# A graph network's residual layer: one gather table first and the other behind it, rows turned early, and the last node batches rearranged

## The chip, the cores and the metric

The kernel runs on one core of a Trainium2 chip. The core has engines that run beside each other, each with its own queue of instructions: PE multiplies matrices (PEld is its loading of weights), DVE works on vectors, ACT evaluates functions and copies, POOL here issues gathers (indirect DMAs), SP issues the other DMAs. The metric is the device time of one execution in microseconds (us); lower is better.

## The reference, cut to what matters

There are 6250 nodes of 128 features and 100000 edges, sorted by destination.

```python
msg_in = jnp.concatenate([node_features[src], node_features[dst], edge_features], axis=1)
h = jax.nn.silu(msg_in @ mW1 + mb1)
messages = h @ mW2 + mb2
aggregated = jax.ops.segment_sum(messages, dst, num_segments=N)
upd_in = jnp.concatenate([node_features, aggregated], axis=1)
u = jax.nn.silu(upd_in @ uW1 + ub1)
updated = u @ uW2 + ub2
return layer_norm(node_features + updated, ln_g, ln_b)
```

The output is `layernorm(x + that)`.

## The kernel before

**Tables.** The first matrix of an edge's message acts on three pieces: the source's features, the destination's features and four edge attributes. So the kernel makes two tables over all nodes: A (`tab_a`), x times the first half of mW1, and B (`tab_b`), x times the second half plus the bias. The nodes are 49 tiles of 128; `parts` puts eight tiles in a part, six full parts and one of a single tile. For each part, `turn_x` transposes x on PE (line 321) and ACT copies the result to `xT` (line 322); then, for four tiles at a time, PE multiplies with both halves at once (line 336, 256 columns), ACT copies A's half to a buffer `t` of which there are two (line 338), DVE adds the bias to B's half and writes it over x (line 339), and SP writes both to memory (lines 342 and 343). The PSUM tiles of this stage come from a pool `wide` of three. After the loop come the destination lists (`destination_lists`, lines 211 to 251: transposes on PE, small DVE work, flags) and edge attributes.

**Edges.** Edges are worked on in 98 groups of 1024 (the last has 672), eight tiles of 128 each. `fetch` has POOL issue one gather for each tile of a group (line 268). The gathered rows lie in a ring `gath` of AHEAD + 2 = 6 buffers, and POOL takes them in order of the groups. The first RAW = 4 groups gather rows of x itself, since no table is there yet; from group 4 on rows of A are gathered, which must wait for all of A.

For a group g the edge loop does this:

- SP loads a window of 96 rows of B and the four attribute rows (`load`, lines 525 and 526): the matrix `mv` and the lower rows of `st`.
- DVE writes the upper rows of `st`, a one-hot of the destination (`node_matrix`, line 530), and `oh`, the same by edges (`edge_matrix`, line 543).
- PE multiplies `st` and `mv` (`products`, line 555), which gives B's and the attributes' share.
- From group 4 on, DVE adds the gathered A rows (`hidden`, line 575) and ACT applies silu (line 576). For the first four groups `hidden` transposes the raw rows on PE (line 568), DVE copies them out (line 570), and `products` multiplies them with the first half of mW1 beside line 555 (line 559); ACT applies silu straight from PSUM (line 571). A raw buffer of the ring is free as soon as line 568 has read it.
- PE sums h over the destinations with `oh` (`by_nodes`, lines 582 and 585), and DVE adds that to `acc` and to the counts `deg` (`add`, line 591).

PE, DVE, ACT and SP run their instructions in the order in which the program writes them (`manual_schedule`).

**Nodes.** `node_batch` is a generator that carries a batch of node tiles through the update and both norms in steps, one step per group; `advance` moves all running batches by one step. A batch starts once the sums of its nodes are complete. The tiles are cut from the front into eleven batches of four, one of three, and a last one of two, which alone waits for the final group:

```python
for i0, n in groups(NT - 2, BT):
    batches.append((i0, n, (i0 + n) * P * E // (N * GE) + 1))
batches.append((NT - 2, 2, NG))
```

In a batch ACT copies its part of `acc` and `deg` (lines 433 and 435), PE multiplies (438 to 440), ACT applies silu (443), PE multiplies again (445, 454), and DVE and ACT do the two norms (456 to 483; the square root is line 425). Silu and square root lie in different function tables of ACT, which have to be loaded at each switch. In the last iterations both running batches take their steps in turn, the older one first.

Of the kernel before, what the change touches and what calls it, by code (L numbers as in the profile page):

```python
# [18 lines left out]
P = 128  # L19
# [5 lines left out]
def kernel(  # L25
# [46 lines left out]
    G = 8  # L72
# [24 lines left out]
    def groups(n, g):  # L97
        return [(i, min(g, n - i)) for i in range(0, n, g)]


    batches = []
    for i0, n in groups(NT - 2, BT):
        batches.append((i0, n, (i0 + n) * P * E // (N * GE) + 1))
    batches.append((NT - 2, 2, NG))

    edges = ExitStack()
    edges.enter_context(tc.manual_schedule(engines={ENG.SP, ENG.PE, ENG.DVE, ENG.Activation}))
# [210 lines left out]
    def turn_x(i0, n):  # L318
        pt = wide()
        for i in range(n):  # L320
            nc.tensor.transpose(pt[:, i, :], x_sb[:, i0 + i, :], ident)
        nc.scalar.copy(xT[:, i0 * P : (i0 + n) * P], pt[:, :n, :].rearrange("p i f -> p (i f)"))

    parts = groups(NT, G)
    turn_x(*parts[0])
    for k, (i0, n) in enumerate(parts):
        if k + 1 < len(parts):
            turn_x(*parts[k + 1])

        tb = x_sb[:, i0 : i0 + n, :]  # L330
        ta = tpool.tile([P, G, H], F32, name="t", bufs=2)
        for j0, m in groups(n, G // 2):
            pm = wide().rearrange("p (i s) f -> p i s f", s=2)
            for j in range(m):
                cols = slice((i0 + j0 + j) * P, (i0 + j0 + j + 1) * P)
                nc.tensor.matmul(pm[:, j], xT[:, cols], w1, start=True, stop=True)  # L336
            own = slice(j0, j0 + m)
            nc.scalar.copy(ta[:, own], pm[:, :m, 0, :])
            nc.vector.tensor_add(
                tb[:, own], pm[:, :m, 1, :], b1[:, None, :].to_broadcast([P, m, H])  # L340
            )
        nc.sync.dma_start(by_node(tab_b)[:, i0 : i0 + n, :], tb)
        nc.sync.dma_start(by_node(tab_a)[:, i0 : i0 + n, :], ta[:, :n])
        cols = slice(i0 * P, NW if i0 + n == NT else (i0 + n) * P)
        nc.vector.memset(acc[:, cols], 0.0)
        nc.vector.memset(deg[:, cols], 0.0)
# [3 lines left out]
    destination_lists()  # L350
    attribute_rows(0)
    destinations(0)
    if E < NG * GE:
        pad = tpool.tile([ED, NG * GE - E], F32, name="pad")
        nc.vector.memset(pad, 0.0)
        nc.sync.dma_start(ea_d[:, E:], pad)
# [42 lines left out]
        nc.scalar.copy(mb2u, pm[0:1, 2, :])  # L399


    def node_batch(i0, n, work, new, y):

        cols = slice(i0 * P, (i0 + n) * P)
        m = (min((i0 + n) * P, N) - i0 * P) // n
        assert m * n == min((i0 + n) * P, N) - i0 * P

        def rows_of(t):

            return t[i0 * P : i0 * P + m * n].rearrange("(p j) f -> p j f", j=n)  # L410

        def flat(t):
            return t[:, :n].rearrange("p i f -> p (i f)")

        def moments(v):
            mv = work.tile([P, BT, 2], F32, name="mv", bufs=2)
            for i in range(n):
                st = work.tile([P, 6], F32, name="st", bufs=2)
                nc.vector.bn_stats(st, v[:, i, :])  # L419
                nc.vector.bn_aggr(mv[:, i, :], st)  # L420
            return mv

        def std(mv):
            r = work.tile([P, BT], F32, name="r", bufs=2)
            nc.scalar.activation(r[:, :n], mv[:, :n, 1], AF.Sqrt, bias=eps)  # L425
            return r

        xs = new("xs")
        if m < P:
            nc.vector.memset(xs[m // 32 * 32 :, :n], 0.0)  # L430
        nc.sync.dma_start(xs[:m, :n], rows_of(x))
        acc_b = new("acc_b")
        nc.scalar.copy(flat(acc_b), acc[:, cols])
        deg_b = new("deg_b", 1)
        nc.scalar.copy(flat(deg_b), deg[:, cols])
        yield
        y = y()
        nc.tensor.matmul(flat(y), u1x, xT[:, cols], start=True, stop=False)
        nc.tensor.matmul(flat(y), w2u, flat(acc_b), start=False, stop=False)
        nc.tensor.matmul(flat(y), mb2u, flat(deg_b), start=False, stop=True)  # L440
        yield
        uT = new("uT")
        nc.scalar.activation(flat(uT), flat(y), AF.Silu, bias=ub1_col)
        yield
        nc.tensor.matmul(
            y[:, :n],
            ones[0:1, :],
            ub2_row[:, None, :].to_broadcast([1, n, H]),
            start=True,
            stop=False,  # L450
        )
        by_p = flat(uT).rearrange("k (p j) -> k p j", j=n)
        for i in range(n):
            nc.tensor.matmul(y[:, i, :], by_p[:, :, i], u2, start=False, stop=i == n - 1)  # L454
        yield
        nc.vector.tensor_add(y[:, :n], y[:, :n], xs[:, :n])
        mv = moments(y)
        nc.vector.tensor_add(xs[:, :n], xs[:, :n], b_b[:, None, :].to_broadcast([P, n, H]))
        yield
        r = std(mv)  # L460
        yield
        nc.vector.reciprocal(r[:, :n], r[:, :n])
        z = new("z")
        for i in range(n):
            nc.vector.scalar_tensor_tensor(  # L465
                y[:, i, :], y[:, i, :], mv[:, i, 0:1], g_b, op0=OP.subtract, op1=OP.mult
            )
            nc.vector.scalar_tensor_tensor(  # L468
                z[:, i, :], y[:, i, :], r[:, i : i + 1], xs[:, i, :], op0=OP.mult, op1=OP.add
            )  # L470
        mz = moments(z)
        yield
        rz = std(mz)
        yield
        nc.vector.reciprocal(rz[:, :n], rz[:, :n])
        shift = work.tile([P, BT], F32, name="shift", bufs=2)
        nc.vector.scalar_tensor_tensor(  # L477
            shift[:, :n], mz[:, :n, 0], -1.0, rz[:, :n], op0=OP.mult, op1=OP.mult
        )
        yield  # L480
        o = z
        for i in range(n):
            nc.scalar.activation(  # L483
                o[:, i, :], z[:, i, :], AF.Identity, bias=shift[:, i : i + 1], scale=rz[:, i : i + 1]
            )
        yield
        nc.sync.dma_start(rows_of(out), o[:m, :n])
# [60 lines left out]
        )  # L548
        return oh

    def products(g, xg=None):
        pre = rows_ps()
        st = stbuf[g % NST].rearrange("k (i c) -> k i c", i=G)
        for i in range(tiles_of(g)):
            nc.tensor.matmul(  # L555
                pre[:, i, :], st[:, i, :], mv[g % NM], start=True, stop=xg is None
            )
            if xg is not None:
                nc.tensor.matmul(pre[:, i, :], xg[:, i, :], w1[:, 0, :], start=False, stop=True)  # L559
        return pre  # L560

    def hidden(g):
        h = hbuf[g % NH]
        ga = rows.pop(g)
        if g < RAW:
            px = rows_ps()
            for i in range(G):
                nc.tensor.transpose(px[:, i, :], ga[:, i, :], ident)  # L568
            xg = work.tile([P, G, P], F32, name="s")
            nc.vector.tensor_copy(xg, px)  # L570
            nc.scalar.activation(h, products(g, xg), AF.Silu)  # L571
        else:
            n = tiles_of(g)
            s = work.tile([P, G, H], F32, name="s")
            nc.vector.tensor_add(s[:, :n], ga[:, :n], pre.pop(g)[:, :n])  # L575
            nc.scalar.activation(h[:, :n], s[:, :n], AF.Silu)  # L576
        return h

    def by_nodes(g, h, oh):
# [14 lines left out]
        load(g)  # L594
    for g in range(MADE):
        node_matrix(g)
    pre, oh, h, pt, running = {}, {0: edge_matrix(0)}, {}, {}, []
    for g in range(NG + 1):
        if g == 3:
            load_weights()  # L600
        if g == 5:
# [7 lines left out]
            fetch(g + AHEAD)  # L609
        if g + LEAD < NG:  # L610
            load(g + LEAD)
        if g == RAW:
            for k in (g, g + 1):
                pre[k] = products(k)
        last = g >= NG - 1
        if not last:
            h[g] = hidden(g)
        if g >= RAW and g + 2 < NG:
            pre[g + 2] = products(g + 2)
        if g + MADE < NG:  # L620
            node_matrix(g + MADE)
# [4 lines left out]
                add(k, pt.pop(k))  # L626
        if not last:
            pt[g] = by_nodes(g, h.pop(g), oh.pop(g))
        for i0, n, first in batches:
            if g == min(first + 1, NG):  # L630
                tiles = node_tiles(nodes, node_y)
                if first == NG:

                    tiles = (
                        nodes,
                        lambda name, p=P: gath.tile([P, G, H], F32, name="ga")[:p, :BT],
                        lambda: rows_ps()[:, :BT],
                    )
                running.append(node_batch(i0, n, *tiles))
        advance(running)  # L640
        if g >= NG - 2:
            advance(running)
        if g == NG - 1:
            pt[g] = by_nodes(g, hidden(g), oh.pop(g))
    while running:
        advance(running)
    edges.close()
# [155 lines left out]
```

## Time and profile before

| what | us |
|---|---|
| median of three runs | 1023.12 (1022.43 to 1024.61) |
| the profiled execution's own time | 1023.03 |
| its span, first to last instruction | 1021.3 |
| POOL busy in it | 741.8 |
| PE busy | 685.0 |
| DVE busy | 477.2 |
| ACT busy | 238.2 |
| end of the raw gathers on POOL | 43.94 |
| first gather from A | 52.24 |
| last gather issued | 992.31 |
| last output issued | 1015.68 |

All times in the text are counted from the start of the span. The page's groups have one row for each line of the kernel, engine and operation, with busy time, mean duration and the idle time before it. A wait is named with the instruction that waited and the one that ended it.

### The profile page before, as it was taken

To read this page: it belongs to the slowest core of one execution; us is meant where nothing else is said; L and a number is where in the kernel's file an instruction comes from. 1 tells how busy PE (TensorE), PEld (TensorE's weight loads), DVE (VectorE), ACT (ScalarE), POOL (GpSimd) and SP (SyncE) were. 2 spreads that over 40 slices of the span, in tenths; PEclk is the share of its full clock that TensorE was granted. 3 is DMA by queue.
4 is the path that set the end of the run, shared out by engine and by line. 5 is a ranking of instruction groups with operands and counts; after the bars stand their busy time and mean duration, and the time that the engine had idled before them with its cause. 6 is when DMAs were issued, how large, how long until landed. Compare 5 with 4: busy or idle time off the path is not lost.

```text
span 1021.3 us, 11233 instructions
## 1 busy us (share of the span) xinstructions
PE 685.0 (67%) x3696; PEld 618.4 (61%) x3696; DVE 477.2 (47%) x1018; ACT 238.2 (23%) x294; POOL 741.8 (73%) x790
## 2 busy tenths in 40 slices
PE   5748896658667677657547765767667666647763
PEld 4637886547556676556546664666666565647652
DVE  3752765434534444542543453452544453453454
ACT  2311231221231131131222232122222132123134
POOL 6577777777777777777777777777777777777760
PEclk9957997686587657767787777767767767776665
DMA  8943342232323322323233224233232332222220
GB/s 214 288 118 93 90 116 58 77 92 75 86 74 84 83 78 55 93 77 94 60 90 87 65 66 110 62 90 83 68 86 73 85 84 71 75 78 68 53 57 31
DMA packets 69916, 88.95 MB, mean 87 GB/s; under 512 B 20671, under 2 KB 51534, under 8 KB 69850
## 3 DMA queue, kind: packets, MB, share of 16 engines
q0 software_dynamic: 25024, 51.30, 20.0%
q1 hardware_dynamic: 41290, 35.08, 11.9%
q10 hardware_dynamic: 3536, 1.77, 0.7%
q8 instruction: 31, 0.51, 0.2%
q14 instruction: 35, 0.29, 0.1%
HBM read 76.71 MB, written 11.38 MB: 86 GB/s over the span
## 4 chain that ended last, share of the span: by engine, by line
POOL 53%; issue 24%; DMA 7%; DVE 6%; PE 4%; ACT 1%; DVEq 0%; POOLq 0%; ACTq 0%
POOL ga L268 53%; DMA ga<-tab_a,src_i 7%; PE pt L585 1%; PE pre L555 1%; DVE st L530 1%; DVE z L468 1%; DVE oh L543 1%; DVE y L465 1%; PE pre L559 1%; DVE st L419 1%; DVE mv L420 1%; PE pre L568 0%; DVE s L570 0%; ACT h L571 0%; DVE s L575 0%
## 5 line engine op out<-in xcount | busy, mean ns | idle before, releaser
L268 POOL DMA_INDIRECT ga<-tab_a,src_i x750 | 710.5, 947 | 237.9 <-issue 216.7
L555 PE MATMUL pre<-mv,st 100*128 100x128 f32 x1564 | 319.0, 382 | 277.3 <-DVE s L575 223.9
L555 PEld LDWEIGHTS pre<-mv,st 100*128 100x128 f32 x1564 | 293.2, 286 | 299.0 <-DVE s L575 243.0
L575 DVE TENSOR_TENSOR s<-ga,pre 128x1024 f32<-128x1024 f32 x94 | 114.4, 1217 | 469.7 <-DMA ga<-tab_a,src_i 450.5
L576 ACT ACTIVATE h<-s 128x1024 f32<-128x1024 f32 x94 | 99.1, 1055 | 661.7 <-DVE s L575 661.6
L585 PE MATMUL pt<-oh,h 128*128 128x96 f32 x1564 | 247.9, 326 | 5.5 <-ACT h L571 5.5
L585 PEld LDWEIGHTS pt<-oh,h 128*128 128x128 f32 x1564 | 243.5, 245 | 12.4 <-ACT h L571 6.6
L530 DVE TENSOR_SCALAR_CACHE_REDUCE st<-near,p_next 96x1024 f32<-96x1024 uint8 x98 | 124.2, 1269 | 1.7 <-DMA ea_d<-pad 1.7
L543 DVE TENSOR_TENSOR oh<-w_row,rel 128x768 f32<-128x768 f32 x98 | 92.9, 948 | 0.0
L582 PE MATMUL pt<-ident,deg_g 96*1 96x96 f32 x98 | 32.0, 327 | 9.1 <-DVE deg L591 8.9
L425 ACT ACT_TABLE_LOAD x24 | 30.8, 1283 | 2.7 <-DVE mv L420 2.3
L454 PEld LDWEIGHTS y<-u,uT 128*128 128x128 f32 x94 | 22.7, 327 | 10.4 <-issue 10.4
L268 POOL DMA_INDIRECT ga<-in_x_dram,src_i x24 | 22.6, 944 | 7.3 <-issue 7.3
L576 ACT ACT_TABLE_LOAD x21 | 26.9, 1283 | 0.4
L591 DVE TENSOR_TENSOR acc<-acc,pt 128x96 f32 x98 | 23.6, 241 | 4.9 <-PE pt L585 4.9
L454 PE MATMUL y<-u,uT 128*128 128x128 f32 x94 | 25.8, 429 | 0.0
L336 PE MATMUL wide<-w,xT 128*128 128x256 f32 x98 | 24.1, 403 | 0.0
L591 DVE TENSOR_TENSOR deg<-deg,pt 1x96 f32 x98 | 23.1, 235 | 0.0
L336 PEld LDWEIGHTS wide<-w,xT 128*128 128x128 f32 x98 | 19.5, 205 | 2.9
L420 DVE BATCH_NORM_AGGREGATE mv<-st 128x2 f32<-128x6 f32 x98 | 17.8, 182 | 3.4
L483 ACT ACTIVATE z<-z,shift,r 128x128 f32<-128x128 f32 x47 | 19.2, 479 | 0.4 <-DVE shift L477 0.4
L559 PE MATMUL pre<-w,s 128*128 128x128 f32 x64 | 16.0, 341 | 4.8 <-DVE s L570 4.8
(117 smaller groups left out, 343.2 us busy)
## 6 DMA issues: line engine op xcount, KB each, us to landing
ga<-tab_a,src_i POOLq DMA_INDIRECT x750
near<-near_d SPq DMA_DIRECT2D x24, 384.0 KB
mv<-tab_b SPq DMA_DIRECT2D x98, 48.0 KB
tab_b<-x_sb SPq DMA_DIRECT2D x6, 512.0 KB
tab_a<-t SPq DMA_DIRECT2D x6, 512.0 KB
xs<-in_x_dram SPq DMA_DIRECT2D x11, 256.0 KB
out_dram<-z SPq DMA_DIRECT2D x11, 256.0 KB
st<-ea_d SPq DMA_DIRECT2D x98, 16.0 KB
```

Source lines behind the costliest of these rows:

```text
L268: nc.gpsimd.indirect_dma_start(out=rows[g][:, i, :], out_offset=None, in_=x if g < RAW else tab_a[:, :], in_offset=bass.IndirectOffsetOnAx ...
L336: nc.tensor.matmul(pm[:, j], xT[:, cols], w1, start=True, stop=True)
L425: nc.scalar.activation(r[:, :n], mv[:, :n, 1], AF.Sqrt, bias=eps)
L454: nc.tensor.matmul(y[:, i, :], by_p[:, :, i], u2, start=False, stop=i == n - 1)
L530: nc.vector.tensor_scalar(stbuf[g % NST][:W], near.pop(g), p_next, 0.0, op0=OP.is_equal, op1=OP.add, accum_out=deg_g[:, g : g + 1],)
L543: nc.vector.tensor_tensor(oh, w_row[:, None, :].to_broadcast([P, G, W]), rel[:, g, :, None].to_broadcast([P, G, W]), op=OP.is_equal,)
L555: nc.tensor.matmul(pre[:, i, :], st[:, i, :], mv[g % NM], start=True, stop=xg is None)
L575: nc.vector.tensor_add(s[:, :n], ga[:, :n], pre.pop(g)[:, :n])
L576: nc.scalar.activation(h[:, :n], s[:, :n], AF.Silu)
L582: nc.tensor.transpose(pt[0:1, W:], deg_g[:, g : g + 1], ident[:W, :W])
L585: nc.tensor.matmul(pt[:, :W], h[:, i, :], oh[:, i, :], start=i == 0, stop=i == n - 1)
L591: nc.vector.tensor_add(at, at, of)
```

## The change

It has four parts.

1. The loop over parts makes only A, 128 columns a tile. Destination lists and attributes follow, and then a second loop makes B for all parts.
2. In that second loop, `turn_rows` transposes the raw rows of groups 0 to 3 and writes them back over the gathered rows. `products` reads them from there, and the raw groups' products are made two groups ahead, like the others'.
3. The batches are cut so that the first has one tile, eleven have four, and the last two have two each. From NG - 6 on, all running batches take two steps in a group.
4. After the loop the last batch (`final`) reads `acc` and `deg` directly, and goes ahead of the batch before it in every round of steps.

```diff
+    LAST = 2
     batches = []
-    for i0, n in groups(NT - 2, BT):
+    first = (NT - 2 * LAST) % BT
+    for i0, n in [(0, first)] * (first > 0) + [
+        (first + i, n) for i, n in groups(NT - 2 * LAST - first, BT)
+    ] + [(NT - 2 * LAST, LAST)]:
         batches.append((i0, n, (i0 + n) * P * E // (N * GE) + 1))
-    batches.append((NT - 2, 2, NG))
+    batches.append((NT - LAST, LAST, NG))
...
+    def table(i0, n, half):
+        pm = wide()
+        for j in range(n):
+            cols = slice((i0 + j) * P, (i0 + j + 1) * P)
+            nc.tensor.matmul(pm[:, j, :], xT[:, cols], w1[:, half, :], start=True, stop=True)
+        return pm[:, :n, :]
+
+    def turn_rows(g):
+
+        px = wide()
+        for i in range(G):
+            nc.tensor.transpose(px[:, i, :], rows[g][:, i, :], ident)
+        nc.vector.tensor_copy(rows[g], px)
+
     turn_x(*parts[0])
     for k, (i0, n) in enumerate(parts):
         if k + 1 < len(parts):
             turn_x(*parts[k + 1])
-
-        tb = x_sb[:, i0 : i0 + n, :]
         ta = tpool.tile([P, G, H], F32, name="t", bufs=2)
-        for j0, m in groups(n, G // 2):
...
-        nc.sync.dma_start(by_node(tab_b)[:, i0 : i0 + n, :], tb)
+        nc.scalar.copy(ta[:, :n], table(i0, n, 0))
         nc.sync.dma_start(by_node(tab_a)[:, i0 : i0 + n, :], ta[:, :n])
...
     destinations(0)
+    for k, (i0, n) in enumerate(parts):
+        if k < RAW:
+            turn_rows(k)
+
+        tb = x_sb[:, i0 : i0 + n, :]
+        nc.vector.tensor_add(tb, table(i0, n, 1), b1[:, None, :].to_broadcast([P, n, H]))
+        nc.sync.dma_start(by_node(tab_b)[:, i0 : i0 + n, :], tb)
...
-        acc_b = new("acc_b")
-        nc.scalar.copy(flat(acc_b), acc[:, cols])
-        deg_b = new("deg_b", 1)
-        nc.scalar.copy(flat(deg_b), deg[:, cols])
+        sums, counts = acc[:, cols], deg[:, cols]
+        if not final:
+
+            acc_b, deg_b = new("acc_b"), new("deg_b", 1)
+            nc.scalar.copy(flat(acc_b), sums)
+            nc.scalar.copy(flat(deg_b), counts)
+            sums, counts = flat(acc_b), flat(deg_b)
...
-    def products(g, xg=None):
+    def products(g):
         pre = rows_ps()
         st = stbuf[g % NST].rearrange("k (i c) -> k i c", i=G)
         for i in range(tiles_of(g)):
...
+            nc.tensor.matmul(pre[:, i, :], st[:, i, :], mv[g % NM], start=True, stop=g >= RAW)
+            if g < RAW:
+                nc.tensor.matmul(
+                    pre[:, i, :], rows[g][:, i, :], w1[:, 0, :], start=False, stop=True
+                )
         return pre
...
-    pre, oh, h, pt, running = {}, {0: edge_matrix(0)}, {}, {}, []
-    for g in range(NG + 1):
+    oh, h, pt, running = {0: edge_matrix(0)}, {}, {}, []
+    pre = {g: products(g) for g in range(2)}
+    for g in range(NG):
...
-        if g >= RAW and g + 2 < NG:
+        if g + 2 < NG:
             pre[g + 2] = products(g + 2)
...
+        for _ in range(2 if g >= NG - 6 else 1):
+            if not last:
+                advance(running)
+
+    g = NG - 1
+    advance(running)
+    before = running[-1]
+    next(before)
+    pt[g] = by_nodes(g, hidden(g), oh.pop(g))
+    next(before)
+    add(g, pt.pop(g))
+    final = node_batch(
...
+        final=True,
+    )
+    for _ in range(2):
+        next(final)
+    running = [final, before] + running[:-1]
     while running:
         advance(running)
```

## The prediction

> **What bounds the kernel now.** I read the page's chain of waits first, then its groups, then the waits of POOL alone, then the timeline of the first 125 us and of the last 50.
>
> ```profile
> POOL 53%; issue 24%; DMA 7%; DVE 6%; PE 4%; ACT 1%; DVEq 0%; POOLq 0%; ACTq 0%
> L268 POOL DMA_INDIRECT ga<-tab_a,src_i x750 | 710.5, 947 | 237.9 <-issue 216.7
> ...
> POOL ga L268 <- DMA mv<-in_L_gnn_mW_dram: 8.3, 1, 8.3
> POOL ga L268 <- PE pre L568: 1.5, 1, 1.5
> ```
>
> POOL issues 782 gathers, 0.944 us each and 0.30 to the next: 1.25 us, 977 us in all, nearly the whole span. From 4 us on it stops only twice for more than 0.5 us: 8.29 us until table A has landed, and 1.46 us (1.16 more than the usual 0.30) until buffer 3 of its ring of six is free. So the time is: when POOL starts group 6 (the first group that reuses a buffer) + 92 groups + the tail after the last gather. I price the change in these terms.
>
> ```profile
> 43.00 0.94 POOL L268 DMA_INDIRECT ga<-in_x_dram,src_i  x1 [0.30 <-issue]
> 52.24 0.94 POOL L268 DMA_INDIRECT ga<-tab_a,src_i  x1 [8.29 <-DMA mv<-in_L_gnn_mW_dram]
> ...
> 72.21 0.94 POOL L268 DMA_INDIRECT ga<-tab_a,src_i  x1 [0.30 <-issue]
> ...
> 994.99 0.95 DVE L575 TENSOR_TENSOR s<-ga,pre 128x768 f32<-128x768 f32 x1 [0.18 <-DMA ga<-tab_a,src_i]
> ...
> 1000.84 0.26 DVE L591 TENSOR_TENSOR acc<-acc,pt 128x96 f32 x1 [4.90 <-PE pt L585]
> ...
> 1009.48 0.43 DVE L456 TENSOR_TENSOR pre<-pre,ga 128x256 f32<-128x256 f32 x1
> ...
> 1015.34 0.34 SPq L487 DMA_DIRECT2D out_dram<-ga  x1
> ```
>
> The reader sees the raw gathers end at 43.94, the tables' gap, group 6 at 72.21 with no wait (buffer 0 was freed by the transposes of line 568 at 56.87 to 58.84), and a tail of 20 us after the last data.
>
> **What the skill says.** "TensorE: Matmul & The Clock Gate", Part 1: the PE runs at half clock until a free-running window of 3413 ns has been busy. The trace agrees: the clock is 0.50 or 1.00, and in half-microsecond slices it switches near 47.87, 71.77, 75.18 and 88.84, whole multiples of 3.41 apart. Its Part 4 says of transposes that the full clock does not engage for them. The trace has one stretch that tests this, the first line here (columns: the stretch, its length, then PE, PEld, DVE, ACT and POOL busy, clock, DMA share, GB/s):
>
> ```profile
> 78.20:81.60 3.40, 3.26 (x16) 2.97 (x15) 0.53 (x1) 0.00 (x0) 2.54 (x3) 0.50 0.23 57
> 81.60:85.00 3.40, 2.65 (x12) 2.65 (x13) 2.76 (x4) 0.00 (x0) 2.49 (x4) 0.50 0.14 40
> 85.00:88.40 3.40, 3.40 (x18) 3.40 (x17) 0.00 (x0) 0.00 (x0) 2.51 (x3) 0.50 0.21 58
> 88.50:92.00 3.50, 2.47 (x20) 2.18 (x20) 0.00 (x0) 2.00 (x2) 2.76 (x3) 0.95 0.23 58
> ```
>
> 78.2 to 81.6 was 96% busy, over half of it transposes (79.1 to 81.0), and the clock stayed at half; 85.0 to 88.4, matmuls alone and busy throughout, raised it. That supports the page, with one sample. "DMA: Bandwidth & Descriptors", Anatomy of one DMA, gives about 2.0 us fixed for a transfer; here an st load issued until 63.07 lets PE go at 65.07. "ScalarE: Activation LUTs", What ACT_TABLE_LOAD costs, gives 1283 ns; the page's 24 loads have that mean.
>
> **Part 1: A alone in the first loop.** Before, a part of 8 tiles takes PE 1.04 (transposes) + 3.32 (256 columns) and the parts follow at 4.33 us. At 128 columns a tile takes 0.22 at full clock, 0.43 at half (the pairs of lines 555/559 at 72 and 68 us), so a part takes 1.04 + 1.75 = 2.8. The first A runs at half clock to 20.1 as now; five more periods end PE's share near 34 instead of 43.6. ACT has two copies of 1.01 a part and keeps up. An A tile's buffer waits for the write two parts back: 512 KB at some 235 GB/s (287 moved from 24 to 43.6 us, less 52 for gathers of 64 KB in 1.25 us) is 2.2 + 2.0 us, with the copy some 5.4 for two parts, no limit. The last A is then issued near 38 and lands near 40.5, before POOL comes at 44.25. **The 8.29 gap falls to 0.30: -8.0**, and groups 4 and 5 end at 64.2.
>
> **Part 2: what group 6 waits for now.** In the changed order of instructions POOL's first gather of group 6 waits for PE and DVE: raw rows are turned in place, so buffer 0 is read until the last matmul of products(0). That needs mv, which needs all of B. Before, it needed only line 568. The chain:
> - The destination lists come to PE at 34 instead of 48.65, with the same 8.2 us to the last small transpose (48.65 to 56.87): 42. DVE's memsets and subtracts are done by then; bad_i ends 3.3 us later, 45.7, batches one longer (0.15).
> - The B stretch is 4 x 8 transposes and 49 matmul tiles on PE: 4 x 1.04 + 49 x 0.22 = 14.9 at full clock, 4 x 1.91 + 49 x 0.43 = 28.7 at half. It starts cold (idle since 36). DVE has 4 copies and 7 adds of some 1.2 (line 570; two adds of 0.65 before) and is under PE.
> - Turns and tables alternate: 1.91 of transposes, 3.42 of matmuls. If transposes count as busy, PE is at full clock after at most two windows: end near 59. If they don't, a window needs 3.0 to 3.4 us of pure matmuls out of a period of 5.3, and gets it only by phase; surely only in parts 4 to 6, which have no turns: end near 69.
> - From there 1.3 to the last big add, then its 512 KB behind the write before: 4.5 to 5.5. SP's mv and st issue and land in 2.85 (62.27 to 65.07 and the wake). products(0) is 16 tiles, PE cold again: 6.0 (between 3.5 and 6.8).
> - Sum: 59 + 1.3 + 5 + 2.85 + 6 = 74 at best, 69 + 1.3 + 5 + 2.85 + 6 = 84. I take 80: the window may fit by phase in the middle of the stretch.
>
> Group 6 then starts at 80 instead of 72.21: **+7.8**, of which -1.3 comes back: the waits of 1.16 at 93.33 and 0.17 at 113.47 go, as products(1) to (3) follow within POOL's 10 us a group. **Net start +6.5**, range -1.5 (T = 72) to +13. Queued behind the waiting gather are only later gathers, and their data are not missed: PE, DVE and ACT still have groups 0 to 5 to work through. But POOL never catches up what it stood, since every group costs it 10 us to the end.
>
> SP is moved past nothing it waits long for: mv, ea, near_d stand between A and B, all issued by 46, the first B at 48. The middle of the loop costs nothing: POOL runs five buffers ahead there, some 40 us of cover.
>
> **Part 3: the tail.** Before: h of group 97 at 997.40 behind four z activations, pt until 1000.8, then two ACT copies of 0.41 and 0.40, silu behind two table loads (1004.77), matmuls to 1007.66, and DVE reaches the last batch only at 1009.48, held by the three-tile batch. After: acc and deg feed PE directly, two tiles instead of three, silu of the last batch ahead of the other's sqrt. From the waits of the order: h(96) pays one table load of 1.28 behind its s, since the load carries that wait; the middle batch's y ends near 995.8 (3 x 0.63), its second matmuls near 998.2, pt(97) at 1000.6, add 0.3, two matmuls 1.3, silu 1002.3, matmuls 1005.1. The middle batch's sqrt follows with a load, 1004.4, its normalisation 2.45: 1006.9. So DVE takes the last batch at 1007.0 (now 1009.48), 6.35 to the output instead of 5.86, for the shared engine: 1013.35 against 1015.34. **-2.0**, from -1.3 to -3 by how warm PE is. After that 5.96 us to the end, unchanged.
>
> **Sum:** 1023.03 (profiled; span 1021.3; median 1023.12, no different) + 6.5 - 2.0 = **1027.6**.
>
> **Rivals.**
> - *The turn counts for the clock* or the window fits early: group 6 near 73.7, 1023.1 + 0.2 - 2.0 = 1021.3 (1019.5 to 1023.5). For: only one sample says otherwise, and the A loop of before kept full clock with a quarter of its time in transposes. Against: that sample and the page.
> - *No new wait*: buffer 0 free by 64.2: 1023.1 - 8.0 - 1.3 - 2.0 = 1011.8. It decides if products(0) ends before 64.2, 10 us sooner than my best sum; against it stands that B alone holds PE 14.9 us after 42.
> - *The A loop loses its clock too*, as its matmul runs are now 3.42 and not 6.9: PE's parts take 5.3, A's end 50, and all that follows is later by up to 16; partly hidden by POOL's raw gathers, group 6 near 90 to 95: about 1037. Against: at 16.7 to 20.1 the first run alone sufficed, and a window of that length needs only a lucky phase.
> - *It doesn't do what it says*: the order shows A, then B; left at 3%.
>
> **How the numbers follow.** Forecast 0.57 (1024.6 to 1033.6), clock rival 0.25, no new wait 0.07, A cold 0.08, other 0.03. A measurement tells 0.2%, 2.05 us: faster is under 1021.1, slower over 1025.2. Faster: 0.4 of the clock rival and the no-wait case, 0.18; same: the rest of the clock rival, the forecast's edge, other, 0.20; slower 0.62. Range 1020.5 to 1035 leaves out the no-wait case, a quarter of the clock rival and most of the cold A: 0.19. The forecast's own is 1024.6 to 1033.6.
>
> **What would show it.** No gap at 44; a POOL wait of some 16 us at group 6, put down to PE's line 574; clock 0.50 through most of 42 to 64; the last B issued near 70; the last output issued 18.3 us after the last s starts, where it is 1015.34 - 994.99 = 20.35 now. Group 6 before 74 would make me wrong in the main step, and a tail within 1 us of the old one in the third.

## The result and the profile after

The changed kernel took 1020.81 us (median of 14 runs, 1018.05 to 1022.80) against 1022.72 for the kernel before in the same sitting: the ratio is 0.9981, 95% interval 0.9973 to 0.9990. The forecast was 1027.6. The changed kernel is a little faster where it was forecast slower, and the time is close to that of the rival in which transposes count for PE's clock (1021.3).

The profiled execution took 1018.05 us, its span 1016.1: the fastest of the 14, some 2.8 us under their median. So the sum below explains this execution, and the spread is looked at further below. First the chain of waits on the page, with the gathers' row of the page's groups (busy us, mean ns; then POOL's idle time before them):

```profile
POOL 55%; issue 26%; DMA 5%; PE 4%; DVE 3%; ACT 1%; SPq 1%; DVEq 0%; POOLq 0%; ACTq 0%
...
L272 POOL DMA_INDIRECT ga<-tab_a,src_i x750 | 710.5, 947 | 235.2 <-issue 220.9
```

The gathers still carry the span, at the same price each. In the waits of POOL (total, times, longest) the table's 8.3 us are gone and one new wait stands in their place:

```profile
POOL ga L272 <- PE pre L574: 6.9, 1, 6.9
```

The timeline has it by place (start, duration, and in brackets the idle time before):

```profile
43.28 0.94 POOL L272 DMA_INDIRECT ga<-in_x_dram,src_i  x1 [0.30 <-issue]
44.53 0.94 POOL L272 DMA_INDIRECT ga<-tab_a,src_i  x1 [0.30 <-issue]
...
71.08 0.94 POOL L272 DMA_INDIRECT ga<-tab_a,src_i  x1 [6.89 <-PE pre L574]
...
992.50 0.95 DVE L587 TENSOR_TENSOR s<-ga,pre 128x768 f32<-128x768 f32 x1 [0.51 <-DMA ga<-tab_a,src_i]
...
997.78 0.26 DVE L603 TENSOR_TENSOR acc<-acc,pt 128x96 f32 x1 [0.92 <-PE pt L597]
...
1004.12 0.41 DVE L473 TENSOR_TENSOR pre<-pre,ga 128x256 f32<-128x256 f32 x1
...
1010.09 0.35 SPq L504 DMA_DIRECT2D out_dram<-ga  x1
```

Table A is there in time: the first gather from it follows the last raw one with the usual 0.30 us. POOL then stands 6.89 us at group 6, on the last matmul of products(0), as the forecast said it would; but group 6 starts at 71.08, not at 80, and 1.13 us before the old 72.21. The sum for the two spans, 1021.3 to 1016.1 (s is what DVE makes of a group's gathered rows and its products):

| term | us |
|---|---|
| group 6 starts at 71.08 instead of 72.21 | -1.13 |
| from there to the last s: 921.42 instead of 922.78 (the later waits gone) | -1.36 |
| from the last s to the last output: 17.59 instead of 20.35 | -2.76 |
| sum | -5.25 |

What PE did in the stretch that decides, from its timeline:

```profile
38.84 1.93 PE L341 MATMUL wide<-ident,ga 128*128 128x128 f32 x8
40.56 2.97 PE L334 MATMUL wide<-w,xT 128*128 128x128 f32 x16
43.37 1.04 PE L341 MATMUL wide<-ident,ga 128*128 128x128 f32 x8
...
49.86 5.75 PE L334 MATMUL wide<-w,xT 128*128 128x128 f32 x50
64.27 0.77 PE L572 MATMUL pre<-mv,st 100*128 100x128 f32 x2 [8.66 <-DMA st<-ea_d]
```

Only the first turn takes 1.93 us; from the second on eight transposes take 1.04 us, which is full clock. PE is through with B at 55.6 and then has nothing to do for 8.66 us, until B has landed and its rows have been loaded. products(0) starts cold at 64.27 and its last matmul is what frees buffer 0.

### The profile page after: what moved, and what is told of

It reads as the page before. It is cut to its first block, busy times and chain, and to the rows that moved or that the text cites. A ratio compares the mean times of both kernels' runs of the same rounds, so it can differ in the third digit from the quotient of the medians.

```text
span 1016.1 us, 11475 instructions
## 1 busy us (share of the span) xinstructions
PE 698.9 (69%) x3802; PEld 640.0 (63%) x3802; DVE 477.5 (47%) x1018; ACT 239.6 (24%) x293; POOL 742.3 (73%) x790
## 4 chain that ended last, share of the span: by engine, by line
POOL 55%; issue 26%; DMA 5%; PE 4%; DVE 3%; ACT 1%; SPq 1%; DVEq 0%; POOLq 0%; ACTq 0%
POOL ga L272 55%; DMA ga<-tab_a,src_i 5%; PE pre L572 1%; PE pt L597 1%; PE pre L574 1%; DVE z L485 0%; DVE y L482 0%; DVE st L547 0%; DVE st L433 0%; DVE mv L434 0%; SPq L526 0%; DVE oh L560 0%; DVE s L587 0%; SPq L542 0%; ACT L439 0%
## 5 line engine op out<-in xcount | busy, mean ns | idle before, releaser
L572 PE MATMUL pre<-mv,st 100*128 100x128 f32 x1564 | 331.9, 394 | 277.2 <-DVE s L587 216.8
L572 PEld LDWEIGHTS pre<-mv,st 100*128 100x128 f32 x1564 | 304.5, 296 | 299.3 <-DVE s L587 237.2
L597 PEld LDWEIGHTS pt<-oh,h 128*128 128x128 f32 x1564 | 252.0, 252 | 7.7 <-ACT h L588 1.2
L597 PE MATMUL pt<-oh,h 128*128 128x96 f32 x1564 | 255.6, 333 | 0.9 <-ACT h L588 0.9
L334 PE MATMUL wide<-w,xT 128*128 128x128 f32 x196 | 25.9, 292 | 0.1
L334 PEld LDWEIGHTS wide<-w,xT 128*128 128x128 f32 x196 | 25.1, 209 | 0.6 <-ACT xT L326 0.3
L485 DVE SCALAR_TENSOR_TENSOR z<-y,r,xs 128x128 f32<-128x128 f32 x47 | 16.5, 350 | 1.7
```

The source lines that it names most:

```text
L334: nc.tensor.matmul(pm[:, j, :], xT[:, cols], w1[:, half, :], start=True, stop=True)
L572: nc.tensor.matmul(pre[:, i, :], st[:, i, :], mv[g % NM], start=True, stop=g >= RAW)
L597: nc.tensor.matmul(pt[:, :W], h[:, i, :], oh[:, i, :], start=i == 0, stop=i == n - 1)
```

## The experiments

The first eight ran in two sittings of four, in which the kernel before took 1022.71 and 1022.80 us. The edits shown are to the changed kernel, but for the second, which is to the kernel before. Ratios are to the kernel before, and intervals are of 95%.

**1. The start alone.** Parts 1 and 2 of the change, with the batches and the tail of before.

```diff
-    LAST = 2
     batches = []
-    first = (NT - 2 * LAST) % BT
...
+    for i0, n in groups(NT - 2, BT):
         batches.append((i0, n, (i0 + n) * P * E // (N * GE) + 1))
-    batches.append((NT - LAST, LAST, NG))
+    batches.append((NT - 2, 2, NG))
```

> The first half of the change alone: table A first, B behind it, raw rows turned in that stretch; batches and the end of the loop as before. Theory S (the 8.3 us that POOL waited for table A have become a wait of group 6 for the products of group 0, and its length follows the PE clock): no wait for A, one wait of 5 to 12 us ahead of group 6, group 6 starting between 70 and 77 us where it was 72.21; time within 2 us of before (1021 to 1025), with a spread of some 3 to 4 us between runs. Rival G (the start brings the gain, and the profiled run shows its usual size): group 6 at 71, time 2 to 3 us under before. Rival L (as forecast, the clock stays at half while rows are turned): group 6 near 80, time 4 us or more over before.

Measured: 1021.49 us, 0.9989 (0.9982 to 0.9996). Its profile has group 4 at 44.65 and group 6 at 71.04, after a wait of 6.72 us on the same matmul, and its time from the last add to `acc` to the last output is that of the kernel before, 14.50 us. So the start brings about 1.2 us instead of the 6.5 that it was forecast to cost.

**2. The tail alone.** Parts 3 and 4, with the start of before.

```diff
+    LAST = 2
     batches = []
-    for i0, n in groups(NT - 2, BT):
+    first = (NT - 2 * LAST) % BT
...
+        final=True,
```

> The other half alone: two batches of two tiles at the end, the last one reading the sums directly and going in front, two steps a group in the last groups; the start as before. Theory S: the gain of the whole change is made here, 2.8 us: last output issued 17.6 us after the last addition of gathered rows starts (before 20.35), time near 1020. Rival G: under 1 us.

Measured: 1019.47 us, 0.9975 (0.9964 to 0.9986): -3.2 by the medians, -2.6 by the ratio. In its profile the last output is issued 17.51 us after the last s, near the 17.6 that was expected. Start and tail alone add up to more (-4.4 by the medians, -3.7 by the ratios) than both together (-1.9), but each carries some 0.7 to 1.2 us of uncertainty. Whether the two take something from each other stays open.

**3. A ring of eight buffers.** The changed kernel with two more buffers for gathered rows.

```diff
-    gath = edges.enter_context(tc.tile_pool(name="gath", bufs=AHEAD + 2))
+    gath = edges.enter_context(tc.tile_pool(name="gath", bufs=AHEAD + 4))
```

> The changed kernel with eight buffers in the ring of gathered rows instead of six, so that groups 6 and 7 need no buffer of groups 0 and 1. Theory S: the wait ahead of group 6 goes, group 6 starts at 64.3, group 8 finds its buffer free at 84; time 1011.5 (1010 to 1013), and the spread between runs shrinks, as the PE clock no longer sets when POOL goes on. Rival: products of groups 1 to 3 come too late as well and the wait turns up ahead of group 8 with 5 us or more; time 1016 or more.

Measured: 1013.56 us, 0.9905 (0.9892 to 0.9919), a little over the 1010 to 1013 that was expected. The timeline of POOL shows group 6 without a wait:

```profile
64.73 0.94 POOL L272 DMA_INDIRECT ga<-tab_a,src_i  x1 [0.30 <-issue]
```

So the new wait is all that kept the removed gap from being a gain: once no gather needs buffer 0 before products(0) has read it, the 7 us are there. The kernel before with eight buffers wasn't run; its only waits for a buffer are the 1.16 and 0.17 us that the prediction names. The spread did not shrink as was expected (1011.37 to 1014.29, 2.9 us in five runs): with the start's wait gone, something else still varies.

**4. All of B ahead of the turns.**

```diff
     for k, (i0, n) in enumerate(parts):
-        if k < RAW:
-            turn_rows(k)
-
         tb = x_sb[:, i0 : i0 + n, :]
...
+    for k in range(RAW):
+        turn_rows(k)
```

> The changed kernel with all of table B made ahead of the four turns instead of between them. Theory W (PE stands idle from 55.6 to 64.3 for B's way through memory, so turns belong into that idle time): B's matmuls end near 52 instead of 55.6, its writes follow one another at the rate of memory and land near 59.5 instead of 61.3, products of group 0 begin near 62.5, group 6 near 69; time 1.5 to 3 us under the changed kernel. Rival M (the writes of B are bound by memory from the first on): B lands no earlier than 61, time within 1 us of the changed kernel.

Measured: 1017.87 us, 0.9951 (0.9938 to 0.9964). From the timeline:

```profile
39.44 12.96 PE L334 MATMUL wide<-w,xT 128*128 128x128 f32 x98
...
44.41 11.19 SPq L363 DMA_DIRECT2D tab_b<-x_sb  x7
...
52.24 1.04 PE L341 MATMUL wide<-ident,ga 128*128 128x128 f32 x8
...
60.88 0.35 SPq L541 DMA_DIRECT2D mv<-tab_b  x1
...
69.44 0.94 POOL L272 DMA_INDIRECT ga<-tab_a,src_i  x1 [5.26 <-PE pre L573]
```

PE has B ready at 52.24, 3.4 us before the changed kernel's 55.6, yet the first load from B is issued at 60.88 instead of 61.35, only 0.47 sooner. So PE isn't what B waits for at full clock. The writes are: from the first of them to the first load it is 16.5 us here, 15.8 in the changed kernel and 14.8 to 17.0 in the eight profiles with B behind A, for the same 3.2 MB (six writes of 512 KB and one of 64). In the changed kernel's stretches (length; PE, PEld, DVE, ACT and POOL busy; clock, DMA share, GB/s) the DMA engines are busy 91% or more of each stretch from 46 to 60, and stay so after PE has ended:

```profile
46.00:48.00 2.00, 2.00 (x21) 2.00 (x20) 2.00 (x3) 0.00 (x0) 1.66 (x2) 1.00 0.94 260
...
56.00:58.00 2.00, 0.00 (x0) 0.00 (x0) 1.20 (x3) 0.00 (x0) 1.64 (x2) 1.00 1.02 301
58.00:60.00 2.00, 0.00 (x0) 0.00 (x0) 0.00 (x0) 0.00 (x0) 1.44 (x2) 0.94 1.05 307
60.00:62.00 2.00, 0.00 (x0) 0.00 (x0) 0.72 (x1) 0.00 (x0) 1.39 (x2) 0.50 0.56 152
```

The rest of this kernel's 1.64 us at group 6 is the clock's phase: products(0) took its first 5.7 us at half clock in the changed kernel (64.27 to 69.99), here its first 3.4 (63.73 to 67.2). The median lies 2.9 us under the changed kernel's, more than the 0.47 us by which B comes sooner; the one profile doesn't show what makes up the rest.

**5. All turns ahead of B.** The disputed step by itself: 32 transposes with no table matmul among them.

```diff
+    for k in range(RAW):
+        turn_rows(k)
     for k, (i0, n) in enumerate(parts):
-        if k < RAW:
-            turn_rows(k)
-
         tb = x_sb[:, i0 : i0 + n, :]
```

> The changed kernel with the four turns of raw rows (32 transposes) ahead of all tables of B, instead of one turn ahead of each of the first four. If transposes count as busy time for PE's clock, the clock goes from 0.50 to 1.00 while PE is still transposing: the 32 transposes start near 38.8 us, the rise comes at 42.3 to 45.7, by a whole 3.41 us of nothing but transposes, PE's last table ends near 56 as in the changed kernel, and the first B tile is written some 3 us later. The last B write is then later by up to 3 us if the writes' rate bounds it, so that group 6 starts at 71 to 75 and the whole is +0 to +3 us on the changed kernel: 1020 to 1024. If they don't count (the theory on record), the 32 take 7.7 us at half clock until 46.5, the clock rises only at 50 or later, by a whole window of table matmuls, PE ends near 63, group 6 starts at 80 or later, and the whole is near 1028.

Measured: 1025.22 us, 1.0025 (1.0017 to 1.0033). The question it was made for is answered by the stretch of one clock window (columns as above) and PE's timeline:

```profile
37.93:41.34 3.41, 3.15 (x16) 3.15 (x17) 2.05 (x19) 1.09 (x1) 2.67 (x3) 0.50 0.55 135
41.34:44.76 3.42, 2.00 (x16) 1.52 (x14) 2.71 (x5) 0.00 (x0) 2.51 (x4) 1.00 0.70 152
```

```profile
38.31 4.27 PE L341 MATMUL wide<-ident,ga 128*128 128x128 f32 x24
43.91 0.76 PE L341 MATMUL wide<-ident,ga 128*128 128x128 f32 x5 [1.34 <-DVE ga L342]
46.62 0.93 PE L341 MATMUL wide<-ident,ga 128*128 128x128 f32 x3 [1.95 <-DMA ga<-in_x_dram,src_i]
47.39 4.81 PE L334 MATMUL wide<-w,xT 128*128 128x128 f32 x27
```

From 37.93 to 41.34 PE was busy 3.15 of 3.41 us, 3.03 of them with these transposes, and the clock rose to full at its end, in the midst of the 24. Transposes count. The time itself is a miss (1020 to 1024 was expected): the second wait is for the last raw gather, which POOL issues only at 44.30, so the last three transposes can't begin before 46.6, and standing ahead of B they take all of B with them. The first write of B comes at 51.60 instead of 45.54 and group 6 at 76.23. The order in the change hides that landing behind two parts of B; this kernel's loss is mostly that wait. The clock, back at half from 48.15 to 51.57, adds about 1 us (the first 16 table matmuls take 2.93 us, where 16 take 1.95 in the changed kernel at full clock).

**6. Both: B ahead and a ring of eight.**

```diff
-    gath = edges.enter_context(tc.tile_pool(name="gath", bufs=AHEAD + 2))
+    gath = edges.enter_context(tc.tile_pool(name="gath", bufs=AHEAD + 4))
...
     for k, (i0, n) in enumerate(parts):
-        if k < RAW:
-            turn_rows(k)
-
...
+    for k in range(RAW):
+        turn_rows(k)
```

> All tables of B ahead of the turns and a gather ring of eight buffers instead of six, both in one. If the ring takes group 6's wait away altogether, moving B ahead has nothing left to bring at the start: 1013.5, as the ring of eight alone (1012.5 to 1014.5). If the gains add (the ring 7.3, B ahead 2.9), 1010.5. The first is expected: group 6 at 64.7, groups 8 and later without a wait over 0.5 us.

Measured: 1012.77 us, 0.9911 (0.9898 to 0.9924): as the ring alone. With two more buffers, an earlier B brings nothing that shows.

**7. The last batch behind the one before it.**

```diff
-    running = [final, before] + running[:-1]
+    running = running[:-1] + [before, final]
```

> The changed kernel with the last batch's steps behind those of the batch before it in the rounds after the loop, as they stood before. The start is untouched: group 6 at 71 to 72.5. If going in front is what shortens the tail, most of the 2.8 us come back: from the last sum of A rows to the last output 19.5 to 20.4 us instead of 17.6 to 18.2, and the whole is +1.5 to +2.5 us on the changed kernel. If it's the direct reading of the sums, or the smaller batches, under 1 us comes back.

Measured: 1017.84 us, 0.9960 (0.9947 to 0.9973), the contrary of what was expected: behind is faster than in front, by 3.0 us in the medians and 2.5 us in the tail of the profiles. The timeline of the changed kernel, last batch in front, shows ACT's silu for the last batch (line 460), its load of the root's table, the root of the batch before (line 439), and DVE's next step with that batch (line 479):

```profile
999.69 0.47 ACT L460 ACTIVATE ga<-pre,ub_col 128x256 f32<-128x256 f32 x1 [5.29 <-PE pre L457]
1000.18 1.28 ACT L439 ACT_TABLE_LOAD   x1
1001.48 0.30 ACT L439 ACTIVATE r<-mv,eps 128x2 f32<-128x2 f32 x1
1001.81 0.17 DVE L479 RECIPROCAL r<-r 128x2 f32<-128x2 f32 x1 [3.24 <-ACT r L439]
```

And with it behind:

```profile
993.89 1.28 ACT L439 ACT_TABLE_LOAD   x1
...
995.96 0.30 ACT L439 ACTIVATE r<-mv,eps 128x2 f32<-128x2 f32 x1 [0.79 <-DVE mv L434]
996.27 1.28 ACT L460 ACT_TABLE_LOAD   x1
997.21 0.25 DVE L603 TENSOR_TENSOR acc<-acc,pt 128x96 f32 x1 [0.97 <-PE pt L597]
998.03 0.17 DVE L479 RECIPROCAL r<-r 128x2 f32<-128x2 f32 x1
...
1001.05 0.43 DVE L473 TENSOR_TENSOR pre<-pre,ga 128x256 f32<-128x256 f32 x1 [0.63 <-PE pre L471]
...
1007.04 0.34 SPq L504 DMA_DIRECT2D out_dram<-ga  x1
```

In front, ACT stands 5.29 us for PE while the other batch's variance is long done, and DVE 3.24 us for that batch's root. Behind, ACT takes the root and nearly both table loads (the second ends at 997.55) while PE still sums the last group (until 997.2), and DVE normalises the other batch while PE makes the last one's products. From the last add to `acc` to the last output it is 9.83 us, against 12.31; in six other profiles with the last batch in front (experiments 2 to 6 and 8) it is 12.38 to 12.80, so this isn't the clock's phase. In the kernel before it was 14.50.

**8. The two copies kept.**

```diff
-        final=True,
```

> The changed kernel with ACT's two copies of the sums and counts kept in the last batch, as in every other. The two copies took 0.41 and 0.40 us before, on the path from the last add to the first matmul of the last batch. If they're only a term of the chain, +0.8 us on the changed kernel, and the tail from the last sum of A rows to the last output is 18.4 instead of 17.6 (same phase of PE's clock). If ACT is also late for the copies, behind the other batch's function, up to +2 us; if PE is late for another reason, 0.

Measured: 1020.44 us, 0.9980 (0.9971 to 0.9989). The same distance, from the last add to the last output, is 12.72 us, within what the profiles without the copies show (12.31 to 12.80). So the copies cost 0.4 us at most and not 0.8: PE starts on the copied sums while ACT copies the counts.

**9. Ring, B ahead and last batch behind together; a ring of seven.** Both in one sitting, and again in another; the first of them three times more by itself, with nearly the same expectation.

```diff
-    gath = edges.enter_context(tc.tile_pool(name="gath", bufs=AHEAD + 2))
+    gath = edges.enter_context(tc.tile_pool(name="gath", bufs=AHEAD + 3))
```

> The changed kernel with a ring of eight, all tables of B ahead of the turns, and the last batch's steps behind those of the batch before it. If the ring takes 8 us from the start and the order of the last two batches takes 2.5 to 3 us from the tail, as each did alone, and the two don't touch each other: 1012.8 - 2.7 = 1010.1 (1009 to 1011.5), with group 6 near 64.6 and the last output issued 15 to 16 us after the last sum of A rows. If the gain in the tail was a lucky phase of PE's clock in that run, the tail is 17.5 to 18.2 us and the whole 1012 to 1013.5.

> The changed kernel with a gather ring of seven buffers instead of six (eight were tried). Group 6 then takes the seventh buffer without a wait, near 64.6 us, and group 7 is the first to reuse one, at 74.6 at the earliest, when products(0) has read it (it ended at 70 to 73). So one more buffer should do all that two did: group 7 without a wait over 1 us, and 1013 to 1014.5. If products(0) comes later than 74.6 in many runs, or the next groups' products fall behind 10 us a group, the ring of eight stays better by 1 us or more.

Neither question could be answered as meant: in all five sittings the kernel before itself took 1306 to 1342 us (medians), and both kernels were slower than it there, by 1.0 to 1.8% and 1.5 to 1.7%. What happened is in the last section. So a best version was not measured beside the other eight; the single gains (the ring -7.3 and the order -3.0 on the changed kernel's median) would make it 1010.6 if they add, which is an estimate.

Two things can still be read there. From the last add to the last output it is 10.28, 11.89, 10.54, 11.89 and 10.32 us in the five profiles with the last batch behind, and 12.59 in both with it in front, so the seventh experiment's finding holds in another condition. And POOL stood 20.7 to 23.2 us at group 4 for table A, and then again: with seven buffers 27.9 us at group 7, where with eight it waited 26.8 at group 8. Under that condition A came late, and B so late that even two more buffers were not enough.

## Why the prediction was wrong

**Part 1, right.** "The 8.29 gap falls to 0.30": it did.

**Part 2, the step that failed.** "Turns and tables alternate ... If transposes count as busy, PE is at full clock after at most two windows: end near 59. If they don't ... end near 69", and of the two "I take 80". They count. The choice rested on one stretch of the trace before, 78.2 to 81.6 us, "96% busy, over half of it transposes", taken as a window in which the clock should have risen. It wasn't a window. The prediction itself gives the switches near 75.18 and 88.84, whole multiples of 3.41 apart; laid out from there, the windows of the kernel before are these:

```profile
78.59:82.01 3.42, 2.87 (x14) 2.58 (x13) 0.94 (x1) 0.00 (x0) 2.69 (x3) 0.50 0.24 58
82.01:85.42 3.41, 3.07 (x14) 3.07 (x15) 2.35 (x4) 0.00 (x0) 2.62 (x3) 0.50 0.20 58
85.42:88.84 3.42, 3.42 (x18) 3.41 (x17) 0.00 (x0) 0.00 (x0) 2.50 (x4) 0.50 0.15 42
```

PE idled from 81.46 to 82.35, across the border, so that one window was 84% busy and the next 90%, and neither raised the clock; the third was full and did. The second of them holds no transpose at all, so transposes aren't needed to explain why the clock stayed. The second experiment's kernel starts as the kernel before does. Its windows lie a little differently over the same work, and the one with the eight transposes (1.92 of its 2.96 busy us) was followed by full clock:

```profile
77.84:81.26 3.42, 2.96 (x14) 2.67 (x13) 0.85 (x1) 0.00 (x0) 2.58 (x3) 0.50 0.25 64
81.26:84.67 3.41, 2.98 (x26) 2.98 (x27) 2.44 (x4) 0.00 (x0) 2.49 (x4) 1.00 0.14 38
```

In the changed kernel the same grid gives a window from 39.27 to 42.68 that is full, its first 1.3 us transposes:

```profile
35.86:39.27 3.41, 0.55 (x3) 0.55 (x4) 2.89 (x6) 0.00 (x0) 2.76 (x3) 0.50 0.74 164
39.27:42.68 3.41, 3.41 (x18) 3.41 (x17) 2.23 (x19) 1.08 (x1) 2.53 (x3) 0.50 0.44 137
42.68:46.10 3.42, 3.38 (x30) 3.14 (x29) 2.94 (x3) 0.00 (x0) 2.51 (x4) 1.00 0.67 182
```

That window alone could be read either way; the fifth experiment's couldn't. The Trainium skill says the opposite for transpose mode ("TensorE: Matmul & The Clock Gate", Part 4), and here the measurement decides; whether these transposes, which the trace records as MATMUL, run in the mode that the page means, it doesn't tell. Its Part 1, a free-running window of 3413 ns, fits every switch looked at; what fills a window is less simple, as the last section shows.

**The size of it.** The forecast had PE start on B at 42 and, for group 6 at 80, end near 65. It started at 38.8, since the list chain took 4.9 us instead of the 8.2 carried over from before (3.2 us early), and needed 16.8 us instead of about 23 (6.1 us). The prediction's own figure for the case that transposes count, 42 to 59, is 17 us. So of the 8.9 us by which group 6 came sooner than 80, some 6 are the clock's and some 3 the list chain's, in the terms of that sum. From PE's end to the first load from B it took 5.75 (1.3 and 5 were forecast), then 2.9 to the first product (2.85) and 6.6 for products(0) (6.0). The terms are right, but the form of the sum is not: at full clock the path runs through B's writes and not through PE's end, as the fourth experiment shows. A sum from the first write, 45.5 + 16 + 2.9 + 6.6, gives 71.

**The new wait, right in kind.** It is where it was put, on line 574, and group 6 does wait for all of B. "Net start +6.5", made of +7.8 at group 6 and -1.3 for the later waits, came out as -2.5 in this profile: -1.13 and -1.36.

**Part 3, right in sign, wrong in its reason.** The term was -2.0 and measured -2.76 in this profile. It was credited to the last batch's silu going ahead of the other's root. The seventh experiment shows that this costs some 2.5 us; leaving the copies out brings 0.4 at most. What is left of the gain after that is with the cut and the pace of the batches, which wasn't tried apart.

**The number of the rival.** The 1021.3 of the rival in which transposes count lies near the median of 1020.81, but its terms were +0.2 for the start and -2.0 for the tail, and the profiled execution has -2.5 and -2.8. Its mechanism is confirmed by the fifth experiment; that its number fits so well is in part luck.

**The spread.** Two things vary from run to run by the window's phase. The four profiles with the same start have group 6 at 70.39, 71.04, 71.08 and 72.57, in the order in which the clock rises for B: at 42.01, 42.69, 42.69 and 44.57. And from the last s to the last add it is 5.0 to 5.5 us where the clock rises during the matmuls ahead of it, but 7.55 in the fourth experiment, where it stayed at half until 999. Together they can carry the 4.7 us between the fastest and the slowest of the 14 runs; that they carry all of it wasn't shown.

## What to carry to other kernels

An early result behind a ring of buffers buys nothing until you have asked what frees the next buffer: here the gap moved 16 gathers on, and two more buffers turned a gain of 2 us into one of 9. To read PE's clock from a trace, lay the windows out from the switches that it shows before judging any stretch. And of two batches that share engines at the end, here the one that was ready had to go first, even though the other was the last.

## What the runs showed that was not expected

- Transposes by matmul with the identity (f32, 128 by 128) raise PE's clock: a window with 3.03 of 3.41 us in them did, and so did one with 1.92 us in them and 1.04 in other matmuls.
- PE's busy share alone doesn't tell whether a window raises the clock. Windows 92% and 87% busy did, 90% and 84% didn't: one sample each, and the ends of PE's records are modelled. But in the kernel before, PE is busy throughout four windows in a row (232.19 to 245.84, mostly lines 555, 585 and 445), and the clock stays at half to their end. Two of them:

```profile
235.60:239.02 3.42, 3.42 (x16) 3.20 (x16) 3.13 (x6) 1.06 (x1) 2.51 (x4) 0.50 0.40 131
239.02:242.43 3.41, 3.41 (x18) 3.33 (x18) 0.00 (x0) 0.00 (x0) 2.50 (x4) 0.50 0.25 70
```

  What else counts stays open. In the ten profiles of kernels that took 1012 to 1025 us, no window less than 86% busy is followed by a rise. So in the fifth experiment, where all but 0.12 us of the window's busy time is transposes, it rose on them in any case.
- In the sittings of the ninth experiment PE often stood between two instructions. The waits of all engines of the combined kernel there (total, times, longest) have PE and its weight loads waiting for nothing that the profile shows:

```profile
PEld pt L596 <- issue: 264.9, 222, 3.2
...
PE pt L596 <- issue: 245.6, 215, 3.2
POOL ga L272 <- DVE s L586: 237.5, 33, 12.0
PE pre L571 <- issue: 214.6, 156, 3.9
```

  The same waits of the sixth experiment's kernel, which differs from it in the order of the last two batches alone:

```profile
PE pre L571 <- issue: 49.8, 11, 6.0
```

  There a matmul took no longer than elsewhere, but in whole stretches one followed another only after 1.4 or 2.1 us, POOL stood for buffers that DVE freed late (237.5 us), and the time was no longer the gathers'. Why stays open, and so does why the changed kernels lose there: the kernel before has no profile from these sittings.
